# Mamba layer and attention layer on one core: fourteen Winograd weight pieces made on VectorE beside two attentions, second layer in pairs of images

## The chip, the cores and the metric

The kernel runs on one core of a Trainium2 chip, in float32. The metric is device microseconds of one execution, as the median of several runs. The engines are named as in the profile: PE is TensorE's matmul and PEld its weight load, DVE is VectorE, ACT is ScalarE, POOL is GpSimd, SP is SyncE, which here only issues DMA transfers.

## The reference

The input `x` is 4 x 512 x 32 x 32: 4 images, 512 channels, 1024 positions. Two layers follow each other, each with a group norm ahead of it and a residual around it.

```python
# layer 0: Mamba over the 1024 positions of each image
x = x + mamba(group_norm(x))
#   xn = layer_norm(tokens); xm, z = split(xn @ W_in)         512 -> 2 x 1024
#   xs = silu(causal_conv4(xm)); dt, Bm, Cm = xs @ W_x ...; dt = softplus(dt @ W_dt + b)
#   for each position: h = exp(dt * A) * h + (dt * xs) * Bm;  y = sum_s h * Cm    16 states
#   out = ((y + xs * D) * silu(z)) @ W_out                    1024 -> 512
# layer 1: attention over positions, between two 3x3 convolutions
x = x + pab(group_norm(x))
#   top, center = conv1x1(x)  (64 channels each);  bottom = conv3x3(x, w_bottom)  512 -> 512
#   map = softmax over all 1024*1024 entries of (center^T top)
#   out = conv3x3(x + map @ bottom^T, w_out)                  512 -> 512
```

## The kernel before

**Layer 0** is cut into 512 units: image `b`, channel block pair `e, h` (8 blocks of 128 channels), state `s` (16). A unit makes the decay `da` on ACT (L837), the product `dbx` of input and B on POOL or otherwise (L864), the scan on DVE (L889), the product with C, `da <- da * cbc`, mostly on POOL (L911) or on DVE (L905), and adds it up over the states by matmuls with the identity on PE into `y` (L918). The rows of B and C come as broadcasts by DMA on SP (`bbc`, `cbc`, 256 KB each). Gates, projections and the norms of the next image lie between the units.

The order is not left to the framework: every operation is a step of a list scheduler (`Plan`), which knows a time for each step, the size of each ring of buffers and a priority `prio` (unit numbers, 0 to 512). It replays the engines on its own clock, takes on each engine the ready step of the lowest priority, and writes the instructions in that order. Steps marked `fill` wait until no other step further than 17.64 behind them in priority is open.

**The weight pieces.** Both 3x3 convolutions are done as Winograd products, F(4) along rows and F(2) along columns: 6 x 4 transformed weight matrices of 512 x 512, kept in DRAM (`ub` for `w_bottom`, `uo` for `w_out`). They are made in layer 0 as fill work: `transform` (L1159) makes one of 16 pieces of a convolution (128 input channels x 128 output channels). On SP it loads the three rows of taps (192 KB each); ACT makes two scaled copies (L1177, L1178); POOL makes three additions on 128 x 768 (L1185, L1191, L1195) and nine on 128 x 256 (L1203 to L1205); SP stores the result in twelve transfers of 128 KB (L1212). The loop over 32 pieces gives the first `t0` = 7 the priority -5 and piece `k` behind them `tg * (k - t0)`, with `tg` = 18.5 units.

**Layer 1** is put in order by the framework from the order in the program. `scores(b)` makes the two 1x1 convolutions (`pt`, L1359), the score matrix (`psc`, L1380), the maximum and the exponentials; `conv3` (L1429) makes a 3x3 convolution: the six rows of transformed inputs in three pairs (1,2), (3,4), (0,5), the temporaries `e` to `l` on ACT and POOL, the sums `rr` and the transformed inputs `v` on DVE (L1488 to L1491), then for each of 24 weight matrices a load of 1 MB on SP into a ring of three buffers (`uw`, tag `u`, L1499) and four matmuls (L1503). `attend(b)` (L1546) has eight steps `k` of eight matmuls (`pat`, L1553), each followed by one DVE operation that adds the result to the normalised image (`xg`, L1566). `finish` adds the residual and stores the output; `last` does that for the last image, woven into its last convolution. `norm(b+1)` normalises the next image; its second half is run inside `attend(b)`. For the last image `by_chunk` makes the first inputs of the output convolution inside the attention, chunk by chunk. In the rest of the text `b1` is the first convolution of image 1 (`ub`) and `o0` the second of image 0 (`uo`); `v_b1` and `uw_b1` are their inputs and weights. The order of images is:

```python
st, rp = scores(0, xg)
for b in range(B):
    xb = conv3(f"b{b}", xg, ub, brow[0])
    ...                       # norm(b + 1) is run inside attend
    attend(b, xg, st, rp, xb, after, chunk)
    ...
    st, rp = scores(b + 1, image[b + 1])
    finish(b, conv3(f"o{b}", xg, uo, brow[1]))
```

Of the kernel before, what the change touches and what calls it, by code (L numbers as in the profile page):

```python
# [8 lines left out]
F32 = mybir.dt.float32  # L9
AF = mybir.ActivationFunctionType  # L10
ALU = mybir.AluOpType
# [4 lines left out]
P = 128  # L16
B, C, HH, WW = 4, 512, 32, 32
L = HH * WW
NCC = C // P
# [8 lines left out]
GS = 16  # L28


PRM = dict(pg=0.53, kt=2, ke=1, ka=-0.68, fl=0, fi=4.6, m0=48, n0=50.77, nl=2.05, c0=61.67, cg=6.03, p0=112, e0=6, eg=4.75, g0=78.98, gg=9.04, o0=13.03, og=5.23, dl=8.5, t0=7, tg=18.5, zl=11.5, f1=1.5)


class Buf:
# [137 lines left out]
def mamba_then_pab_kernel(  # L172
# [25 lines left out]
    nc = tc.nc  # L198
# [44 lines left out]

    NP6, NQ = 6, 4
    ub, uo = (
        [
            dram.tile([NP6, P, NCC, C], F32, tag=f"u_{n}_{q}", name=f"u_{n}_{q}")
# [23 lines left out]
    image = {}  # L273
# [6 lines left out]
    with ExitStack() as l0:  # L280
# [13 lines left out]
        QC = C // 4  # L294
# [932 lines left out]
            conv1_first(d, 0, -17 + 0.1 * d)  # L1227
            alone(silu(0, [d], slice(0, T)), -17 + 0.1 * d)
        params(0, -16, (0,))
        for k in range(2 * NPC):  # L1230
            u, src = ((ub, w_bottom), (uo, w_out))[k // NPC]
            transform(u, src, k % NPC, -5 if k < PRM['t0'] else PRM['tg'] * (k - PRM['t0']))

# [61 lines left out]
    with ExitStack() as l1:  # L1295
# [104 lines left out]

        shape = [P, NCC, TI, WW + 2]

        def by_chunk(name, xg):

            e, f = (
                tp.tile(shape, F32, tag="rt", name=f"{n}_{name}", bufs=4) for n in "ef"
            )
            r = tp.tile([P, 2, *shape[1:]], F32, tag="rr", name=f"rr_{name}_1", bufs=1)
            v = xp.tile([P, NQ, 2, NCC, P], F32, tag="v", name=f"v_{name}_1", bufs=2)

            def chunk(c):
                rows = [xg[:, c, a : a + 4 * TI - 3 : 4, :] for a in range(5)]
                for t, a in ((e, 2), (f, 1)):
                    nc.scalar.activation(t[:, c], rows[a], AF.Copy, scale=-4.0)
                    nc.gpsimd.tensor_add(t[:, c], t[:, c], rows[a + 2])
                nc.vector.tensor_add(r[:, 0, c], e[:, c], f[:, c])
                nc.vector.tensor_sub(r[:, 1, c], e[:, c], f[:, c])
                x = [r[:, :, c, :, a : a + 2 * TJ - 1 : 2] for a in range(4)]
                vq = [
                    v[:, q, :, c].rearrange("p n (i j) -> p n i j", j=TJ) for q in range(NQ)  # L1420
                ]
                nc.vector.tensor_sub(vq[2], x[2], x[1])  # L1422
                nc.vector.tensor_add(vq[1], x[1], x[2])
                nc.vector.tensor_sub(vq[0], x[0], x[2])
                nc.vector.tensor_sub(vq[3], x[1], x[3])

            return v, chunk

        def conv3(name, xg, u, bias, first=None, late=None):  # L1429

# [3 lines left out]
            def rows(a):  # L1434
                return xg[:, :, a : a + 4 * TI - 3 : 4, :]

            def tmp(n):
                return tp.tile(shape, F32, tag="rt", name=f"{n}_{name}", bufs=4)

            def flat(t):  # L1440
                return t.rearrange("p c i x -> p (c i x)")

            def inputs(pair):

                r = tp.tile([P, 2, *shape[1:]], F32, tag="rr", name=f"rr_{name}_{pair[0]}", bufs=1)
                r0, r1 = r[:, 0], r[:, 1]
                if pair == (1, 2):
                    e, f = tmp("e"), tmp("f")
                    nc.scalar.activation(e, rows(2), AF.Copy, scale=-4.0)
                    nc.scalar.activation(f, rows(1), AF.Copy, scale=-4.0)  # L1450
                    nc.gpsimd.tensor_add(e, e, rows(4))
                    nc.gpsimd.tensor_add(f, f, rows(3))
                    nc.vector.tensor_add(r0, e, f)
                    nc.vector.tensor_sub(r1, e, f)
                    return r
                if pair == (3, 4):
                    g, h = tmp("g"), tmp("h")
                    nc.gpsimd.tensor_sub(g, rows(4), rows(2))
                    nc.gpsimd.tensor_sub(h, rows(3), rows(1))
                    kept.extend((g, h))  # L1460
                    for o, w in ((r0, 2.0), (r1, -2.0)):
                        nc.vector.scalar_tensor_tensor(
                            flat(o), flat(h), w, flat(g), ALU.mult, ALU.add
                        )
                    return r
                g, h = kept
                k, l = tmp("k"), tmp("l")
                nc.gpsimd.tensor_sub(l, rows(0), rows(2))
                nc.gpsimd.tensor_sub(k, rows(5), rows(3))
                for o, a, w, s in ((r0, l, 4.0, g), (r1, h, -4.0, k)):  # L1470
                    nc.vector.scalar_tensor_tensor(
                        flat(o), flat(a), w, flat(s), ALU.mult, ALU.add
                    )
                return r
# [1 line left out]
            kept = []  # L1476
            y = [None] * 4
            for pair in PAIRS:
                if first and pair == (1, 2):
                    v = first  # L1480
                else:
                    r = inputs(pair)

                    v = xp.tile([P, NQ, 2, NCC, P], F32, tag="v", name=f"v_{name}_{pair[0]}", bufs=2)
                    rv = r.rearrange("p n c i x -> p (n c i) x")
                    x = [rv[:, :, a : a + 2 * TJ - 1 : 2] for a in range(4)]
                    vq = [v[:, q].rearrange("p n c (i j) -> p (n c i) j", j=TJ) for q in range(NQ)]
                    nc.vector.tensor_sub(vq[2], x[2], x[1])  # L1488
                    nc.vector.tensor_add(vq[1], x[1], x[2])
                    nc.vector.tensor_sub(vq[0], x[0], x[2])  # L1490
                    nc.vector.tensor_sub(vq[3], x[1], x[3])  # L1491
                ns = []
                for k, p in enumerate(pair):
                    m = {}
# [48 lines left out]
                nc.vector.scalar_tensor_tensor(f[3], f[3], 6.0, f[1], ALU.mult, ALU.add)  # L1543
            return y

        def attend(b, xg, st, rp, xb, between, chunk):  # L1546


            for k in range(NCC * NH):
                j, h = divmod(k, NH)  # L1550
                pt = ps.tile([P, C], F32, tag="ps", name=f"pat_{b}_{j}_{h}")
                for m in range(NMC):
                    nc.tensor.matmul(  # L1553
                        pt, st[m][:, 2 * P * j + h : 2 * P * (j + 1) : 2],
                        xb[m // 2][:, m % 2, :],
                        start=(m == 0), stop=(m == NMC - 1),
                    )
# [12 lines left out]
                if h and chunk:  # L1570
                    chunk(j)

        dst = [out[b].rearrange("(c p) h w -> p c (h w)", p=P) for b in range(B)]

# [23 lines left out]
        def finish(b, y):  # L1598

            for j in range(NCC):  # L1600
                o = load_sum(b, j, fp, "f4")
                for rr in range(2):
                    turn_back(b, j, o, y, rr)
                nc.scalar.dma_start(dst[b][:, j, :], o)

        def last(b, xg, v):

            o = [load_sum(b, j, xp, "st") for j in range(NCC)]

# [9 lines left out]
        xg = image[0]  # L1619
        st, rp = scores(0, xg)  # L1620
        for b in range(B):
            xb = conv3(f"b{b}", xg, ub, brow[0])
            after = norm(b + 1) if b + 1 < B else iter(())
            next(after, None)

            v, chunk = by_chunk(f"o{b}", xg) if b + 1 == B else (None, None)
            attend(b, xg, st, rp, xb, after, chunk)
            if b + 1 == B:
                last(b, xg, v)
                break  # L1630
            st, rp = scores(b + 1, image[b + 1])
            finish(b, conv3(f"o{b}", xg, uo, brow[1]))
            xg = image.get(b + 1)


# [55 lines left out]
```

## Time and profile before

| | us |
|---|---|
| three runs | 3073.21, 3081.69, 3087.27 |
| median | 3081.69 |
| the profiled execution | 3079.09 |
| its span in the trace | 3077.3 |
| layer 0, to about | 2044 |
| layer 1 | 1033 |
| mean granted PE clock | 0.972 |

The span runs from the first to the last instruction; 1.8 us lie around it. Layer 0 ends where the last residual sums of image 3 are made (DVE L1069, at 2044.5), and the first matmul of layer 1's first convolution stands at 2059.6. The busy time of each engine is summed over both layers, so its share of the span hides that the layers are limited by different engines; a stage is read in windows. The granted clock is the share of full speed at which PE was allowed to run.

### The profile page before, as it was taken

How to read it: one execution, taken by the hardware profiler on the slowest of the kernel's cores; microseconds unless marked ns; L12 is line 12 of the kernel's file. 1: busy time of each engine (PE TensorE's matmuls, PEld its weight loads, DVE VectorE, ACT ScalarE, POOL GpSimd, SP SyncE). 2: the span in 40 equal slices, each digit the busy share in tenths (PEclk: the TensorE clock that was granted, in tenths of full speed). 3: DMA queues.
4: the chain of work that ended last, by engine and by line, in shares of the span. 5: the costliest groups of instructions: out<-in, count | busy, mean ns of one | idle time of the engine just before them, and what ended most of it. 6: DMA issues, size and time to landing. Idle time of an engine off the chain costs nothing.

```text
span 3077.3 us, 36921 instructions
## 1 busy us (share of the span) xinstructions
PE 2789.0 (91%) x11896; PEld 1669.4 (54%) x11896; DVE 2290.1 (74%) x2989; ACT 1822.0 (59%) x3300; POOL 2125.4 (69%) x1197
## 2 busy tenths in 40 slices
PE   6788789999889999888999968879999999999998
PEld 2556566566666666666666656644444444444444
DVE  4579999888999988989988879985285375346344
ACT  4679878898888888788898879941120030030000
POOL 6989888899978899978889999952151143134222
PEclk9899899999999999999999989999999999999999
DMA  6756455577645577745567654448178458628827
GB/s 183 219 171 210 142 158 155 174 233 241 210 139 173 179 222 239 237 128 162 164 189 222 213 159 140 134 121 319 43 266 316 155 175 317 245 85 312 302 86 260
DMA packets 404537, 600.07 MB, mean 195 GB/s; under 512 B 47192, under 2 KB 246104, under 8 KB 379768
## 3 DMA queue, kind: packets, MB, share of 16 engines
q1 hardware_dynamic: 395536, 583.18, 59.8%
q10 hardware_dynamic: 8648, 14.26, 1.3%
q8 instruction: 95, 1.56, 0.2%
q14 instruction: 98, 0.80, 0.1%
q0 software_dynamic: 160, 0.26, 0.0%
HBM read 500.60 MB, written 96.99 MB: 194 GB/s over the span
## 4 chain that ended last, share of the span: by engine, by line
PE 40%; DVE 12%; ACT 6%; DMA 4%; POOL 4%; issue 3%; SPq 0%; DVEq 0%; POOLq 0%; ACTq 0%
PE m_o L1503 10%; PE m_b L1503 8%; PE pat L1553 7%; DVE da L889 5%; PE y L918 3%; PE po L402 2%; PE psc L1380 2%; PE u L875 2%; DMA uw_b<-u_b 2%; POOL da L911 2%; DVE dbx L889 2%; DVE u L889 1%; PE pz L402 1%; PE pp L728 1%; ACT sc L849 1%
## 5 line engine op out<-in xcount | busy, mean ns | idle before, releaser
L911 POOL TENSOR_TENSOR da<-da,cbc 128x1024 f32<-128x1024 f32 x328 | 773.2, 2368 | 114.7 <-DVE da L889 53.1
L849 ACT ACTIVATE sc<-dtxt,bt_sb 128x256 f32<-128x256 f32 x1312 | 578.1, 499 | 99.3 <-PE u L875 98.5
L837 ACT ACTIVATE da<-dt,a_sb 128x512 f32<-128x512 f32 x656 | 454.1, 716 | 78.8 <-PE y L918 62.8
L864 POOL TENSOR_TENSOR dbx<-dtx,bbc 128x1024 f32<-128x1024 f32 x184 | 434.4, 2373 | 10.6 <-DVE carry_sb L894 4.6
L889 DVE TENSOR_TENSOR_SCAN da<-da,carry_sb,u 128x512 f32<-128x512 f32 x328 | 403.1, 1262 | 42.4 <-PE u L875 40.1
L918 PE MATMUL y<-ident,da 128*128 128x128 f32 x2624 | 366.6, 284 | 72.1 <-POOL da L911 69.9
L889 DVE TENSOR_TENSOR_SCAN da<-da,u 128x512 f32<-128x512 f32 x328 | 397.9, 1213 | 31.0 <-PE u L875 29.0
L875 PE MATMUL u<-ident,sc 128*128 128x128 f32 x2624 | 389.2, 282 | 23.5 <-DVE da L889 14.8
L918 PEld LDWEIGHTS y<-ident,da 128*128 128x128 f32 x2624 | 309.4, 146 | 180.6 <-POOL da L911 132.3
L875 PEld LDWEIGHTS u<-ident,sc 128*128 128x128 f32 x2624 | 314.2, 145 | 113.5 <-issue 34.2
L1503 PE MATMUL m_b<-uw_b,v_b 128*128 128x512 f32 x768 | 337.6, 596 | 17.5 <-issue 8.3
L1503 PE MATMUL m_o<-uw_o,v_o 128*128 128x512 f32 x768 | 334.1, 595 | 4.5 <-DVE v_o L1422 4.1
L402 PE MATMUL pxm<-xt,winc 128*128 128x341 f32 (+4 forms) x768 | 251.0, 470 | 21.7 <-DVE xs L661 10.5
L1503 PEld LDWEIGHTS m_b<-uw_b,v_b 128*128 128x128 f32 x768 | 143.4, 190 | 204.1 <-issue 187.1
L402 PE MATMUL pz<-xt,winc 128*128 128x512 f32 x512 | 244.8, 599 | 8.8 <-DMA winc<-in_w_in_dram 2.5
L837 ACT ACTIVATE u<-dt,a_sb 128x512 f32<-128x512 f32 x368 | 245.5, 681 | 11.9 <-DVE da L889 6.7
L1503 PEld LDWEIGHTS m_o<-uw_o,v_o 128*128 128x128 f32 x768 | 145.6, 191 | 190.2 <-issue 181.7
L918 PE MATMUL y<-ident,dbx 128*128 128x128 f32 x1472 | 215.4, 285 | 36.0 <-DVE dbx L905 24.7
L918 PEld LDWEIGHTS y<-ident,dbx 128*128 128x128 f32 x1472 | 175.7, 147 | 88.2 <-DVE dbx L905 25.8
L1553 PE MATMUL pat<-y_b,st 128*128 128x512 f32 x512 | 221.7, 593 | 0.1
L661 DVE SCALAR_TENSOR_TENSOR xs<-pxm,cw_sb,xs 128x341 f32<-128x341 f32 (+8 forms) x288 | 163.6, 569 | 60.6 <-ACT xs L652 53.6
L1511 ACT ACTIVATE e_b<-m_b 128x512 f32<-128x512 f32 x24 | 14.3, 596 | 316.4 <-PE m_b L1503 300.0
(220 smaller groups left out, 4315.4 us busy)
## 6 DMA issues: line engine op xcount, KB each, us to landing
cbc<-bcd SPq DMA_DIRECT2D x512, 256.0 KB, 3.6
uw_b<-u_b SPq DMA_DIRECT2D x96, 1024.0 KB, 5.1
uw_o<-u_o SPq DMA_DIRECT2D x96, 1024.0 KB, 4.9
bbc<-bcd SPq DMA_DIRECT2D x184, 256.0 KB, 3.9
u_b<-work SPq DMA_DIRECT2D x192, 128.0 KB, 3.0
u_o<-work SPq DMA_DIRECT2D x192, 128.0 KB, 3.4
winc<-in_w_in_dram SPq DMA_DIRECT2D x72, 256.0 KB, 3.7
szd<-sz SPq DMA_DIRECT2D x32, 512.0 KB, 4.0
```

The lines of the kernel that those rows point to most:

```text
L402: lambda k=k, lhs=lhs, rhs=rhs: nc.tensor.matmul(p()[:, at : at + cols], lhs(), rhs(), start=(k == 0), stop=(k == n - 1)),
L661: nc.vector.scalar_tensor_tensor(u()[:, first:end], p()[:, first - k - at + before : n - k + before], cw[k], u()[:, first:end], ALU.mult, ...
L837: nc.scalar.activation(t, dt()[:, j], AF.Exp, scale=a_sb[:, at : at + 1])
L849: nc.scalar.activation(sc()[:, k], dtxt()[:, k], AF.Copy, scale=bt[:, at, s : s + 1])
L864: lambda: nc.gpsimd.tensor_mul(hc(), dtx(), b_bc().to_broadcast([P, 2, T])),
L875: nc.tensor.transpose(u()[:, k * P : (k + 1) * P], sc()[:, k, j, :], ident)
L889: nc.vector.tensor_tensor_scan(ht, *((hc()[:, j], u()) if on_act else (u(), hc()[:, j])), carry_sb[:, j, s : s + 1] if h else 0.0, ALU.mul ...
L911: lambda: nc.gpsimd.tensor_mul(hc(), hc(), c_bc().to_broadcast([P, 2, T])),
L918: nc.tensor.matmul(y[j]()[:, k, :], hc()[:, j, k * P : (k + 1) * P], ident, start=(s == 0 and k == 0), stop=(s == NS - 1 and k == NK - 1), ...
L1380: nc.tensor.matmul(pt, top[:, m * P : (m + 1) * P], center[:, h * T : (h + 1) * T], start=True, stop=True,)
L1503: nc.tensor.matmul(m[q], v[:, q, k, c, :], w[:, c, :], start=(c == 0), stop=(c == NCC - 1 and not extra),)
L1553: nc.tensor.matmul(pt, st[m][:, 2 * P * j + h : 2 * P * (j + 1) : 2], xb[m // 2][:, m % 2, :], start=(m == 0), stop=(m == NMC - 1),)
```

## The change

Three things change.

1. Layer 0 makes 18 of the 32 weight pieces instead of 32 (all 16 of `w_bottom` and `EARLY` = 2 of `w_out`), and `tg`, the distance in units between the priorities of two pieces, goes from 18.5 to 42.
2. Layer 1 goes by pairs of images, (0, 1) and (2, 3): scores, first convolution and attention of both, then the second convolution and the output of both. `by_chunk` is gone; `first_inputs` makes the first inputs of `o0` (or `o2`) ahead of the second attention of the pair. The norm of image 2 is run inside `o1`, behind its first inputs.
3. The other 14 pieces of `w_out` are made by a new function `piece`, seven in `attend(0)` and seven in `attend(1)`, one behind each `xg` from `k` = 1 on. A piece loads the same taps (three loads of 192 KB on SP) into a buffer of the ring of the transformed inputs (`v`, two buffers), makes six operations on 128 x 384 and three on 128 x 768 on DVE, the last three into a buffer of the ring of the weights (`u`, three buffers), and stores four parts of 384 KB on SP.

```diff
-PRM = dict(..., t0=7, tg=18.5, zl=11.5, f1=1.5)
+PRM = dict(..., t0=7, tg=42, zl=11.5, f1=1.5)
...
-    NP6, NQ = 6, 4
+    NP6, NQ, EARLY = 6, 4, 2
...
-        for k in range(2 * NPC):
+        for k in range(NPC + EARLY):
             u, src = ((ub, w_bottom), (uo, w_out))[k // NPC]
             transform(u, src, k % NPC, -5 if k < PRM['t0'] else PRM['tg'] * (k - PRM['t0']))
...
-        def by_chunk(name, xg):
...
+        def piece(k):
+
+            c, part = divmod(k, C // QC)
+            cs = slice(part * QC, (part + 1) * QC)
+            taps = w_out[c * P : (c + 1) * P, :, cs].rearrange("p (y x) o -> p y x o", y=3)
+            t = xp.tile([P, NQ, 2, NCC, P], F32, tag="v", name=f"w_{k}", bufs=2)
...
+            nc.sync.dma_start(g[:, 0], taps[:, 0])
+            nc.sync.dma_start(g[:, NP6 - 1], taps[:, 2])
+            nc.sync.dma_start(mid[:, 0], taps[:, 1])
...
+            dve.tensor_add(r[1], r[0], r[5])
+            stt(r[3], r[5], 4.0, r[0], ALU.mult, ALU.add)
+            dve.tensor_sub(r[2], r[1], m)
+            dve.tensor_add(r[1], r[1], m)
+            stt(r[4], m, -2.0, r[3], ALU.mult, ALU.add)
+            stt(r[3], m, 2.0, r[3], ALU.mult, ALU.add)
+            o = fp.tile([P, NCC, C], F32, tag="u", name=f"wo_{k}", bufs=3)
...
+            dve.tensor_add(o[:, 0], g[:, :, 0], g[:, :, 2])
+            dve.tensor_sub(o[:, 1], o[:, 0], g[:, :, 1])
+            dve.tensor_add(o[:, 0], o[:, 0], g[:, :, 1])
+            for q, part in enumerate((g[:, :, 0], o[:, 0], o[:, 1], g[:, :, 2])):
+                nc.sync.dma_start(uo[q].rearrange("n p c o -> p n c o")[:, :, c, cs], part)
...
-        def attend(b, xg, st, rp, xb, between, chunk):
+        def attend(b, xg, st, rp, xb, between, also):
...
-                if h and chunk:
-                    chunk(j)
+                for job in also[k : k + 1]:
+                    if job is not None:
+                        piece(job)
...
+        left = list(range(EARLY, NPC))
+        half = len(left) // 2
+        st, rp = scores(0, image[0])
+        for a in range(0, B, 2):
+            for b in (a, a + 1):
+                xb = conv3(f"b{b}", image[b], ub, brow[0])
+                also = [None] * (8 - half) + left[b * half : (b + 1) * half] if not a else []
+                after, v = iter(()), None
+                if b == a:
+                    after = norm(b + 1)
+                    next(after)
+                else:
+                    v = first_inputs(f"o{a}", image[a])
+                attend(b, image[b], st, rp, xb, after, also)
+                if b == a:
+                    st, rp = scores(b + 1, image[b + 1])
+            finish(a, conv3(f"o{a}", image[a], uo, brow[1], v))
+            if a + 2 == B:
+                last(a + 1, image[a + 1], None)
                 break
+            y = conv3(f"o{a + 1}", image[a + 1], uo, brow[1], mid=lambda: normed(a + 2))
+            finish(a + 1, y)
+            st, rp = scores(a + 2, image[a + 2])
```

More of the change, by code (lines that the diff above doesn't have):

```diff
@@ L28 @@
 GS = 16
-PRM = dict(pg=0.53, kt=2, ke=1, ka=-0.68, fl=0, fi=4.6, m0=48, n0=50.77, nl=2.05, c0=61.67, cg=6.03, p0=112, e0=6, eg=4.75, g0=78.98, gg=9.04, o0=13.03, og=5.23, dl=8.5, t0=7, tg=18.5, zl=11.5, f1=1.5)
+PRM = dict(pg=0.53, kt=2, ke=1, ka=-0.68, fl=0, fi=4.6, m0=48, n0=50.77, nl=2.05, c0=61.67, cg=6.03, p0=112, e0=6, eg=4.75, g0=78.98, gg=9.04, o0=13.03, og=5.23, dl=8.5, t0=7, tg=42, zl=11.5, f1=1.5)
 class Buf:
@@ L1401, in mamba_then_pab_kernel @@
         shape = [P, NCC, TI, WW + 2]
-        def by_chunk(name, xg):
[L1405 to L1427, printed above, removed]
@@ L1429, in conv3, with spread @@
-        def conv3(name, xg, u, bias, first=None, late=None):
+        def spread(name, p, r):
+            v = xp.tile([P, NQ, 2, NCC, P], F32, tag="v", name=f"v_{name}_{p}", bufs=2)
+            rv = r.rearrange("p n c i x -> p (n c i) x")
+            x = [rv[:, :, a : a + 2 * TJ - 1 : 2] for a in range(4)]
+            vq = [v[:, q].rearrange("p n c (i j) -> p (n c i) j", j=TJ) for q in range(NQ)]
+            nc.vector.tensor_sub(vq[2], x[2], x[1])
+            nc.vector.tensor_add(vq[1], x[1], x[2])
+            nc.vector.tensor_sub(vq[0], x[0], x[2])
+            nc.vector.tensor_sub(vq[3], x[1], x[3])
+            return v
@@ new lines, in tmp, with row_pair, first_inputs @@
+        def tmp(n, name):
+            return tp.tile(shape, F32, tag="rt", name=f"{n}_{name}", bufs=4)
+        def row_pair(name, p):
+            return tp.tile([P, 2, *shape[1:]], F32, tag="rr", name=f"rr_{name}_{p}", bufs=1)
+        def first_inputs(name, xg):
+            r = row_pair(name, 1)
+            ts = []
+            for n, a in (("e", 2), ("f", 1)):
+                t = tmp(n, name)
+                rows = [xg[:, :, k : k + 4 * TI - 3 : 4, :] for k in (a, a + 2)]
+                nc.scalar.activation(t, rows[0], AF.Copy, scale=-4.0)
+                nc.gpsimd.tensor_add(t, t, rows[1])
+                ts.append(t)
+            nc.vector.tensor_add(r[:, 0], *ts)
+            nc.vector.tensor_sub(r[:, 1], *ts)
+            return spread(name, 1, r)
@@ new lines, in piece @@
+        def piece(k):
[3 more added lines that the diff above has]
+            t = xp.tile([P, NQ, 2, NCC, P], F32, tag="v", name=f"w_{k}", bufs=2)
+            t = t.rearrange("p q n c t -> p (q n c t)").rearrange("p (r o) -> p r o", o=QC)
+            g, mid = (t[:, a : a + n].rearrange("p (r x) o -> p r x o", x=3) for a, n in ((0, 3 * NP6), (3 * NP6, 3)))
+            nc.sync.dma_start(g[:, 0], taps[:, 0])
+            nc.sync.dma_start(g[:, NP6 - 1], taps[:, 2])
+            nc.sync.dma_start(mid[:, 0], taps[:, 1])
+            r = [g[:, n].rearrange("p x o -> p (x o)") for n in range(NP6)]
+            m = mid[:, 0].rearrange("p x o -> p (x o)")
+            stt, dve = nc.vector.scalar_tensor_tensor, nc.vector
+            dve.tensor_add(r[1], r[0], r[5])
[5 more added lines that the diff above has]
+            o = fp.tile([P, NCC, C], F32, tag="u", name=f"wo_{k}", bufs=3)
+            o = o.rearrange("p c o -> p (c o)").rearrange("p (q r o) -> p q r o", o=QC, r=8)[:, :, :NP6]
+            dve.tensor_add(o[:, 0], g[:, :, 0], g[:, :, 2])
[3 more added lines that the diff above has]
+                nc.sync.dma_start(uo[q].rearrange("n p c o -> p n c o")[:, :, c, cs], part)
@@ L1434, in rows, with conv3 @@
+        def conv3(name, xg, u, bias, first=None, late=None, mid=None):
             def rows(a):
                 return xg[:, :, a : a + 4 * TI - 3 : 4, :]
-            def tmp(n):
-                return tp.tile(shape, F32, tag="rt", name=f"{n}_{name}", bufs=4)
             def flat(t):
@@ L1443, in inputs @@
             def inputs(pair):
-                r = tp.tile([P, 2, *shape[1:]], F32, tag="rr", name=f"rr_{name}_{pair[0]}", bufs=1)
+                r = row_pair(name, pair[0])
                 r0, r1 = r[:, 0], r[:, 1]
[L1447 to L1455, printed above, removed]
                 if pair == (3, 4):
-                    g, h = tmp("g"), tmp("h")
+                    g, h = tmp("g", name), tmp("h", name)
                     nc.gpsimd.tensor_sub(g, rows(4), rows(2))
@@ L1466, in inputs @@
                 g, h = kept
-                k, l = tmp("k"), tmp("l")
+                k, l = tmp("k", name), tmp("l", name)
                 nc.gpsimd.tensor_sub(l, rows(0), rows(2))
@@ L1478, in conv3 @@
             for pair in PAIRS:
-                if first and pair == (1, 2):
-                    v = first
-                else:
[L1482 to L1491, printed above, removed]
+                if pair == (1, 2):
+                    v = first or first_inputs(name, xg)
+                    if mid:
+                        mid()
+                else:
+                    v = spread(name, pair[0], inputs(pair))
                 ns = []
@@ L1617, in last, with normed @@
                 (nc.scalar, nc.sync)[j % 2].dma_start(dst[b][:, j, :], o[j])
[L1619 to L1629, printed above, removed]
+        def normed(b):
+            for _ in norm(b):
+                pass
+        left = list(range(EARLY, NPC))
[17 more added lines that the diff above has]
+                last(a + 1, image[a + 1], None)
                 break
-            st, rp = scores(b + 1, image[b + 1])
-            finish(b, conv3(f"o{b}", xg, uo, brow[1]))
-            xg = image.get(b + 1)
+            y = conv3(f"o{a + 1}", image[a + 1], uo, brow[1], mid=lambda: normed(a + 2))
+            finish(a + 1, y)
+            st, rp = scores(a + 2, image[a + 2])
 def kernel(**inputs):
```

## The prediction

> **What bounds the kernel now.** I read the busy shares first, then the chain of waits, then windows by stage, because a share is a mean over two layers with different limits. All windows below have the columns: stretch, length, busy PE, PEld, DVE, ACT, POOL, granted PE clock, DMA share, GB/s.
>
> ```profile
> PE 2789.0 (91%) x11896; PEld 1669.4 (54%) x11896; DVE 2290.1 (74%) x2989; ACT 1822.0 (59%) x3300; POOL 2125.4 (69%) x1197
> PE 40%; DVE 12%; ACT 6%; DMA 4%; POOL 4%; issue 3%; SPq 0%; DVEq 0%; POOLq 0%; ACTq 0%
> ```
>
> Over the whole span TensorE leads and POOL looks idle a third of the time. By stage it is otherwise:
>
> ```profile
> 640.00:880.00 240.00, 208.26 (x1161) 146.85 (x1159) 221.12 (x303) 205.67 (x379) 232.01 (x128) 0.96 0.70 214
> 880.00:1120.00 240.00, 227.35 (x1193) 152.43 (x1194) 217.54 (x297) 206.55 (x370) 205.51 (x118) 0.99 0.59 174
> 1120.00:1320.00 200.00, 176.18 (x972) 123.67 (x971) 180.34 (x248) 164.58 (x302) 193.27 (x108) 0.95 0.73 231
> 1560.00:1860.00 300.00, 264.27 (x1467) 181.78 (x1466) 242.85 (x305) 254.22 (x469) 286.81 (x156) 0.95 0.65 199
> 2044.00:3077.00 1033.00, 998.81 (x2405) 444.67 (x2404) 531.20 (x588) 136.63 (x244) 299.70 (x148) 0.99 0.61 218
> 2160.60:2216.30 55.70, 55.66 (x135) 25.74 (x134) 9.56 (x18) 0.47 (x2) 1.27 (x1) 1.00 0.07 25
> ```
>
> In the first layer (to 2044 us) four engines are all over 80% busy, and POOL is the fullest in three stretches, 740 us together (97%, 97%, 96%); between them TensorE is. The second layer (fifth row) is TensorE's alone, 97% busy, only 34 us idle. The last row is the first attention: 55.7 us, TensorE without a gap, VectorE 9.6, DMA 7%. So the change takes work from an engine that is first in part of a balanced stage, and puts it where VectorE and the queues are free but TensorE has no slack.
>
> **What a piece costs now.** POOL's rows (busy, mean ns | idle before):
>
> ```profile
> L1203 POOL TENSOR_TENSOR work<-work 128x256 f32<-128x256 f32 x96 | 70.2, 732 | 0.0
> L1185 POOL TENSOR_TENSOR work<-work 128x768 f32<-128x768 f32 x32 | 58.3, 1822 | 28.8 <-ACT work L1177 27.4 <-DMA u_b<-work 0.9 <-POOL da L911 0.4
> ```
>
> L1204 and L1205 are as L1203, L1191 and L1195 as L1185. A piece is 3 x 1.82 + 9 x 0.730 = 12.0 us of POOL, 1.03 us of ScalarE (two scales of 0.51) and 15 DMA issues on SP. Fourteen gone: 168 us of POOL, 14 of ScalarE, 210 issues at 0.44 us each. The order of instructions keeps pieces 0 to 7 where they are (until about 240 us); of the 24 behind them 10 stay, one of them in image 3.
>
> **The first layer's gain, by stage.** In a stretch where POOL is first, I let it shrink until the next engine has POOL's old share.
> - 640 to 880: pieces take 42.6 us, 14/24 of it goes, 24.9. VectorE stops it first: 221.1/0.967 = 228.7, a gain of 11.3.
> - 1120 to 1320: 21 us go; VectorE 180.3/0.966 = 186.7, gain 13.3.
> - 1560 to 1860: 48 us of pieces, 36 go (one stays); TensorE 264.3/0.956 = 276.4, gain 23.6. Here the mechanism is seen directly: at 1816 two 1.8 us operations and six 0.73 us ones stand ahead of a `dbx` product, VectorE waits 6.2 us for that and TensorE then 11.7 us.
> - Image 0 behind 240 us: about 2. Elsewhere POOL isn't first, but TensorE's waits for POOL's `da` and `dbx` there (240 to 640, 880 to 1120, 1320 to 1560) come to 19.5 + 2.9 + 4.3 = 26.7 us; I take half less the 2, 12.
>
> Sum 50 + 12 = **62 us**, which is 37% of the POOL time removed. The lower bound is the chain: on it, from 920 us to the layer's end, the three wide piece lines and a piece's load have 15.8 + 5.3 = 21 us; scaled by 2 to the part before and by 14/24, 25; less a little for dearer neighbours, 22. The upper bound: all POOL time removed in the three POOL-first stretches (82 us) plus the waits elsewhere, 100. ScalarE's 14 us and SP's issues count nothing: neither is first in any stretch.
>
> **The second layer's cost.** On VectorE a piece has six operations on 128x384 and three on 128x768. No row has these shapes; the nearest, 128x512 at 677 ns and 128x1088 at 1283 ns, give 1.052 ns for an element of a row: 6 x 0.542 + 3 x 0.946 = 6.1 us, 85 us in all. Seven of them (43 us), eight `xg` updates (6.0) and the norm (3.0) are 52 of the attention's 55.7 us: VectorE alone just fits, with no reserve.
>
> But a piece also needs its round trip: its loads go into the ring of the convolutions' inputs (`v`, 2 buffers), its result into that of the weights (`u`, 3 buffers). In the second attention SP has strictly: load piece k, store piece k (four stores, which wait for VectorE), load piece k+1. Each load therefore starts only when VectorE has ended the piece before. A 192 KB load lands 4.3 us after its issue, the third issue comes 0.9 us behind the first: 5.2, then 6.1 of VectorE, 11.3 us. If the loads wait in the DMA queue for the stores, 384 KB each in 512-byte packets (32 ns of one of 16 engines per packet by the busiest window of the trace, 1.6 us a store), up to 13.3. The first piece is done before the first `xg`; six more put the last one's end at about 79 to 90 us after the attention's start, and `w_14` and `w_15` stand on VectorE behind the last `xg`. What is queued behind: TensorE's next matmul is the first of `o0`, its 1 MB of weights come from the very buffer that these stores fill, so 3.4 us for the stores to land and 4.9 for the load follow, TensorE resumes at 87 to 101 us, and idles 32 to 46. I take **36**, near the low end, since DMA is 7% busy there, plus 2 for the restart: behind an 8.3 us gap at 2051 the granted clock was 0.54 for 3.5 us.
>
> In the first attention the next piece's loads stand partly ahead of the stores, so it is tighter: `w_8` and `v_b1` end behind the last `xg`, and the first weights of `b1` stand on SP behind `w_8`'s stores. TensorE has the scores of image 1 (22 us) but part of them waits for `xg`: **9** (bounds 4, one piece's tail; 18, a round trip and a weight load).
>
> Order of pairs: the same matmuls, and in the last image the 4.1 us wait for `v_o` goes: -4. Sum: 36 + 2 + 9 - 4 = **43 us** (28 to 62).
>
> **Two rules weighed.** In the second layer L1489, 128x1024 with two SBUF inputs, takes 3.6 us while POOL works and L1488, the same shape, 1.2 when it doesn't. The Trainium skill, SBUF — State Buffer, "Who interferes with whom", says that such a VectorE operation and a GpSimd one that reads SBUF shut each other out; it speaks against this change, as pieces have two SBUF inputs and POOL makes the next convolution's inputs in the attention. With eight POOL operations of 2.5 us it would add up to 20 us of VectorE time to an attention that is nearly full, and the sum would be about 3080. The first layer's scans, with POOL full, are steady at 1.21 to 1.27 us, so no speed-up of VectorE is counted there.
>
> The Trainium skill, TensorE: Matmul & The Clock Gate, "What's actually happening", lets the clock fall after a few idle microseconds and rise after as long at work; the 0.54 for 3.5 us agrees with it, and by it each long gap costs some 1.7 us instead of my 2 for both.
>
> **Sum.** The profiled execution took 3079.1 us (span 3077.3, 1.8 around it), 2.6 under the median of the runs, 3081.7. 3079 - 62 + 43 = **3060 us**, 0.7% under the median.
>
> **The rivals.**
> 1. *Slower: the first layer isn't bound by POOL.* In image 1 (592 to 1078) VectorE has 444.7 and TensorE 441.6 of 486 us, both 91%, as POOL; the chain gives POOL 4% of the span. Then only the chain's 22 us come back: 3079 - 22 + 43 = 3100. It decides where the gain is under 28. Against it: 97% in three stretches, and waits of 11.7 us with pieces ahead.
> 2. *No change: the attentions cost more*, 62, by 13.3 us a piece or by blocked VectorE operations: 3079 - 62 + 62 = 3079.
> 3. *The whole POOL time comes back*, 100, as the scheduler refills the stretches: 3079 - 100 + 43 = 3022. Against: VectorE and TensorE are at 91% there.
> 4. *It doesn't do what it says*: two pieces lie behind the second attention, not beside it. The 36 count that already; if the first attention is strung out like the second, 46 us idle in each, it is 3079 - 62 + 92 - 4 = 3105.
>
> **How the numbers follow.** About 0.5% (15 us) is what a measurement of this kernel can tell from no change, so faster is under 3066, slower over 3097. Forecast 0.40, own range 3042 to 3078, of it 0.32 faster and 0.08 same; rival 3, 0.15 faster; rival 2, 0.10 same; rival 1, 0.28, of it 0.23 slower and 0.05 same; rival 4's bad end, 0.07 slower. Together 0.47, 0.23, 0.30. The range takes in rivals 1 and 3 with a margin of 7 to 9: 3013 to 3107, leaving out 0.2.
>
> **What would show it.** Right: the layer's end (2044 now) at about 1982; POOL under 90% in the three stretches; second layer about 1076 long, with one TensorE gap of over 30 us behind the second attention that ends on a load of `uw_o` and a smaller one behind the first. Wrong: the layer's end over 2020 (rival 1) or under 1950 (rival 3); a VectorE piece over 9 us (blocked by POOL); no gap behind the second attention.

## The result, and the profile after

The changed kernel takes 3099.66 us (median of 5 runs, 3096.44 to 3105.09), the kernel before 3078.81 (median of 5). The ratio is 1.0065, interval 1.0044 to 1.0086: **slower by about 20 us**. The forecast, 3060 and faster, went the wrong way; the time lies in the range and on rival 1 (3100).

The profiled execution took 3099.67 us, its span is 3097.9. The last residual sum of layer 0 (DVE L1069) stands at 2024.3 where it stood at 2044.5, so layer 0 won **20.2 us**; the rest is 3097.9 - 2024.3 = 1073.6 us long where it was 1032.8, so layer 1 lost **40.8**. The prediction had 62 and 43. The cost was near, the gain was three times too large.

The page of the changed kernel, busy times and the chain:

```profile
PE 2785.9 (90%) x11896; PEld 1663.7 (54%) x11896; DVE 2364.3 (76%) x3097; ACT 1807.3 (58%) x3265; POOL 1963.7 (63%) x1023
PE 45%; DVE 20%; ACT 10%; DMA 6%; issue 4%; POOL 4%; SPq 0%; DVEq 0%; POOLq 0%; ACTq 0%
```

POOL lost 162 us of work, VectorE won 74, as the sums had it. The same windows as before the change, with the second layer last:

```profile
640.00:880.00 240.00, 207.84 (x1136) 143.48 (x1135) 220.09 (x300) 204.11 (x371) 201.11 (x98) 0.95 0.62 192
880.00:1120.00 240.00, 223.91 (x1173) 150.79 (x1172) 211.31 (x288) 198.17 (x354) 182.97 (x97) 0.98 0.51 151
1120.00:1320.00 200.00, 180.12 (x1010) 125.13 (x1007) 186.25 (x258) 169.06 (x310) 177.53 (x88) 0.97 0.70 222
1560.00:1860.00 300.00, 274.03 (x1585) 189.99 (x1584) 265.49 (x339) 271.38 (x503) 286.31 (x143) 0.99 0.63 192
2024.00:3097.00 1073.00, 1003.03 (x2405) 448.95 (x2403) 606.32 (x696) 135.57 (x238) 301.31 (x142) 0.97 0.69 238
```

The first row decides it. From 640 to 880 POOL went from 232.0 us to 201.1, and TensorE, VectorE and ScalarE did no more in these 240 us than before (207.8 for 208.3, 220.1 for 221.1, 204.1 for 205.7). POOL simply stood idle for the 31 us that the pieces had taken. The two rows behind it cancel: a little less work in the second (VectorE 211.3 for 217.5), a little more in the third (186.3 for 180.3). In the fourth row it is otherwise: TensorE 274.0 for 264.3, VectorE 265.5 for 242.9, more work in the same time.

The scans of layer 0 can be counted (two a unit), which gives the time at which each unit is reached. Unit 400, early in image 3, is reached at 1654.0 before and 1655.8 after: no gain in three images, although POOL has 130 us less work on pieces there (225.5 us between 240 and 1560 before, 95.5 after). Between units 400 and 416 the change wins 2.5 us, between 416 and 464 it wins 19.4, and behind 464 nothing.

In layer 1 TensorE's waits, of the kernel changed (us in total, times, longest):

```profile
PE m_o L1518 <- DMA uw_o<-u_o: 34.0, 3, 33.3
PE m_b L1518 <- issue: 8.3, 1, 8.3
PE pm_l L1334 <- DVE mv_l L1328: 7.0, 1, 7.0
PE m_b L1518 <- DMA uw_b<-u_b: 6.8, 4, 5.1
PE pt L1359 <- DVE xg L1581: 3.2, 1, 3.2
```

The first is the gap behind the second attention, the fourth (5.1 of it) and fifth are those behind the first; the second was there before, the third is new and belongs to the order of pairs (see below). The timeline of TensorE at the second attention (start, duration, idle before in brackets):

```profile
2334.55 34.07 PE L1568 MATMUL pat<-y_b,st 128*128 128x512 f32 x79
2401.94 10.08 PE L1518 MATMUL m_o<-uw_o,v_o 128*128 128x512 f32 x16 [33.32 <-DMA uw_o<-u_o]
```

and of SP's queue in the same stretch (start and duration of the issues):

```profile
2343.79 0.95 SPq L1461 DMA_DIRECT2D u_o<-w  x2
2346.31 1.35 SPq L1461 DMA_DIRECT2D u_o<-wo  x2
2348.02 0.38 SPq L1443 DMA_DIRECT2D w<-in_w_out_dram  x1
...
2355.52 0.96 SPq L1461 DMA_DIRECT2D u_o<-w  x2
...
2396.34 83.19 SPq L1514 DMA_DIRECT2D uw_o<-u_o  x24
```

A piece's first stores at 2343.8, the next one's at 2355.5: a piece every 11.7 us. The weights of `o0` go out behind the last stores, at 2396.3, and TensorE, done with the attention at 2368.6, goes on at 2401.9.

### The profile page after: what moved, and what is told of

It is laid out like the page before. It is cut to its first block, busy times and chain, and to the rows that moved or that the text cites. A ratio compares the mean times of both kernels' runs of the same rounds, so it can differ in the third digit from the quotient of the medians.

```text
span 3097.9 us, 36662 instructions
## 1 busy us (share of the span) xinstructions
PE 2785.9 (90%) x11896; PEld 1663.7 (54%) x11896; DVE 2364.3 (76%) x3097; ACT 1807.3 (58%) x3265; POOL 1963.7 (63%) x1023
## 4 chain that ended last, share of the span: by engine, by line
PE 45%; DVE 20%; ACT 10%; DMA 6%; issue 4%; POOL 4%; SPq 0%; DVEq 0%; POOLq 0%; ACTq 0%
PE m_b L1518 10%; PE m_o L1518 10%; DVE da L889 7%; PE y L918 5%; PE po L402 4%; PE pat L1568 4%; PE u L875 3%; ACT sc L849 3%; DVE u L889 2%; PE pxm L402 2%; DVE dbx L889 2%; POOL da L911 2%; ACT da L837 2%; PE psc L1380 2%; PE pp L728 2%
## 5 line engine op out<-in xcount | busy, mean ns | idle before, releaser
L889 DVE TENSOR_TENSOR_SCAN da<-da,carry_sb,u 128x512 f32<-128x512 f32 x328 | 402.4, 1262 | 42.6 <-PE u L875 40.1
L918 PE MATMUL y<-ident,da 128*128 128x128 f32 x2624 | 360.0, 282 | 73.6 <-POOL da L911 70.8
L889 DVE TENSOR_TENSOR_SCAN da<-da,u 128x512 f32<-128x512 f32 x328 | 397.8, 1213 | 20.2 <-PE u L875 19.4
L402 PE MATMUL pxm<-xt,winc 128*128 128x345 f32 (+4 forms) x768 | 258.3, 479 | 34.7 <-DVE xs L661 10.7
L918 PE MATMUL y<-ident,dbx 128*128 128x128 f32 x1472 | 209.1, 281 | 24.6 <-DVE dbx L905 12.3
L402 PEld LDWEIGHTS pxm<-xt,winc 128*128 128x128 f32 x768 | 145.4, 200 | 117.5 <-issue 40.9
```

Of the source, the lines that this page charges most:

```text
L402: lambda k=k, lhs=lhs, rhs=rhs: nc.tensor.matmul(p()[:, at : at + cols], lhs(), rhs(), start=(k == 0), stop=(k == n - 1)),
L889: nc.vector.tensor_tensor_scan(ht, *((hc()[:, j], u()) if on_act else (u(), hc()[:, j])), carry_sb[:, j, s : s + 1] if h else 0.0, ALU.mul ...
L918: nc.tensor.matmul(y[j]()[:, k, :], hc()[:, j, k * P : (k + 1) * P], ident, start=(s == 0 and k == 0), stop=(s == NS - 1 and k == NK - 1), ...
```

## The experiments

Times are medians; the kernel before was run beside each group, so the ratio is the safer number. "Layer 0" and "layer 1" are cut at the last L1069 as above, in one profiled execution each. Executions with the same layer 0 ended it up to 4 us apart (2020.4 and 2024.3 below), and one execution of the first experiment by 6 us in the part that the edit does not touch. So differences of a few us in layer 0 are not read.

| run | us | ratio to before, interval | layer 0 | layer 1 |
|---|---|---|---|---|
| before | 3078.8 | | 2044.5 | 1032.8 |
| the change | 3099.7 | 1.0065 (1.0044 to 1.0086) | 2024.3 | 1073.6 |
| without the work of pieces 28 to 31 | 3060.0 | 0.9954 (0.9936 to 0.9973) | 2030.9 | 1036.1 |
| without the work of pieces 8 to 27 | 3063.7 | 0.9959 (0.9944 to 0.9973) | 2028.7 | 1032.9 |
| pieces closer, 14.5 units | 3087.0 | 1.0035 (1.0021 to 1.0050) | 2055.6 | 1033.1 |
| order of pairs alone | 3068.3 | 0.9969 (0.9953 to 0.9985) | 2042.8 | 1023.6 |
| four pieces on VectorE | 3051.9 | 0.9904 (0.9880 to 0.9928) | 2025.2 | 1025.6 |
| first inputs late | 3071.2 | 0.9974 (0.9960 to 0.9989) | 2020.4 | 1044.6 |
| the change at 18.5 units | 3095.2 | 1.0045 (1.0025 to 1.0064) | 2019.9 | 1074.7 |
| without the work of pieces 8 to 31 | 3049.8 | 0.9901 (0.9879 to 0.9923) | 2017.2 | 1031.6 |
| products moved to POOL, two of four | 3078.3 | 1.0003 (0.9988 to 1.0017) | 2026.5 | 1047.5 |
| products moved to POOL, one of four | 3068.1 | 0.9970 (0.9954 to 0.9986) | 2018.3 | 1048.0 |
| two pieces on VectorE | 3053.5 | 0.9910 (0.9886 to 0.9934) | 2029.9 | 1024.8 |
| one piece on VectorE | 3055.3 | 0.9921 (0.9901 to 0.9942) | 2035.6 | 1025.0 |

**Theory and rival at the start.** "Place": the pieces lie in POOL's idle time in images 0 to 2 and cost only in image 3, where the next image's convolutions and norms are missing. "Amount": each microsecond of POOL is worth the same everywhere.

**1. Pieces of image 3 left out.** The kernel before, with this in `transform`, for `k >= 28`:

```diff
+            if copy:                      # loads and stores stay, ACT and POOL do nothing
+                for rows in (slice(1, 4, 2), slice(2, 5, 2), slice(0, 6, 5)):
+                    for q in range(NQ):
+                        ...  step("SP", ..., dma_start(dst, ends()[:, 0:2, min(q, 2)]))
+                return
```

> The kernel before, with the POOL and ACT work of pieces 28 to 31 left out (their loads and stores stay; the weights stored are the taps themselves). These are the pieces that lie in image 3. Theory 'place' (pieces cost only where no next image fills the other engines, in image 3): layer 0 ends 16 to 21 us earlier than 2044, the time about 3060. Rival 'amount' (each us of POOL work removed is worth the same anywhere, by the result 20 us for 168): 48 us x 0.12, about 6 us, 3073.

14 us faster, and by the units it wins 20 us between 416 and 464 (from 6.3 behind to 14.1 ahead). "Amount" (6 us) is out for these four.

**2. Pieces of images 0 to 2 left out.** The same for `8 <= k < 28`.

> The kernel before, with the POOL and ACT work of pieces 8 to 27 left out (their loads and stores stay), 240 us of POOL work in images 0 to 2; pieces 28 to 31 in image 3 stay. 'Place': no change beyond 8 us, 3071 to 3087. 'Amount': 240 x 0.12, about 29 us, 3050. The prediction's stage sums (37% of what is removed) would give 3079 - 89, about 2990.

12.6 us faster for 240 us of POOL work, 0.05 us per us: against 0.3 for the four above. "Place" had said at most 8, "amount" 29, the prediction's way of reckoning 89. None was right, "place" was nearest. Of the 15.8 us that layer 0 wins here, 10.0 lie ahead of unit 128, in image 0, for which the prediction had about 2; units 192 to 384 take 741.7 us for 744.8. The windows of this run in the stretch of the first row above, and in the next:

```profile
640.00:880.00 240.00, 211.68 (x1155) 147.02 (x1154) 221.01 (x303) 200.50 (x365) 181.82 (x82) 0.96 0.70 216
880.00:1120.00 240.00, 224.60 (x1204) 150.50 (x1203) 217.86 (x297) 207.04 (x372) 175.20 (x79) 0.99 0.57 173
```

POOL from 97% to 76% busy, VectorE unchanged at 92%, the pace unchanged: units 128 to 192 take 224.2 us with the pieces and 222.5 without.

**3. Pieces closer together.** The kernel before with one number changed:

```diff
-PRM = dict(..., tg=18.5, ...)
+PRM = dict(..., tg=14.5, ...)
```

> The kernel before with one number changed, the distance of the pieces' priorities, 18.5 to 14.5: all 32 pieces stay on POOL, but the last has priority 348 and none is left for image 3 (from 384 on). 'Place': layer 0 ends 16 to 21 us earlier, the time about 3060, below both kernels. 'Amount': the same POOL work, 3079. The prediction's reading (POOL full in images 1 and 2) makes it slower, since the pieces stand closer there: 3079 + 10 or more.

This fell against "place" (11 us slower) and went as the prediction's reading had it, and for a reason worth having. Image 3 did win, 23 us between units 384 and 512, but images 0 to 2 lost 33. By units (windows of the kernel before, then of this run; units 32 to 64, 128 to 192, 272 to 304):

```profile
255.00:374.00 119.00, 96.05 (x544) 69.87 (x542) 111.64 (x158) 103.60 (x190) 114.62 (x64) 0.91 0.61 186
631.00:855.00 224.00, 200.83 (x1108) 141.22 (x1106) 205.51 (x278) 189.77 (x351) 216.69 (x119) 0.95 0.75 229
1166.00:1276.00 110.00, 102.58 (x568) 70.33 (x567) 97.68 (x126) 91.08 (x169) 106.37 (x62) 0.98 0.74 236
```

```profile
257.00:385.00 128.00, 96.81 (x546) 69.69 (x545) 112.66 (x159) 105.61 (x195) 121.72 (x69) 0.92 0.63 186
642.00:877.00 235.00, 208.51 (x1115) 141.51 (x1114) 205.40 (x277) 194.85 (x360) 227.03 (x130) 0.95 0.74 226
1194.00:1308.00 114.00, 107.27 (x575) 73.06 (x574) 98.47 (x127) 91.77 (x170) 112.05 (x68) 0.97 0.77 234
```

The same units, 24 us longer (9 + 11 + 4), and POOL busy 23.1 us more (7.1 + 10.3 + 5.7): work *added* to POOL here cost its full time. (Over all units up to 384 it is 32.8 us for 35.7 us more of pieces.) Work *taken away* here (experiment 2) won 2 + 1 + 7 us for 74.6 us of POOL less (20.3 + 32.9 + 21.3). POOL stood at 96 to 97% in these windows, and that reads as a corner, not a slope: more work costs nearly all of its time, less work gives little back. (Each of these kernels also has an order of its own from the scheduler, which no run here holds fixed.)

**4. The order of pairs alone.** The changed kernel with all 32 pieces in layer 0:

```diff
-    NP6, NQ, EARLY = 6, 4, 2        ... tg=42
+    NP6, NQ, EARLY = 6, 4, 16       ... tg=18.5
```

> The changed kernel with all 32 pieces made in layer 0 at the old distance of 18.5 and none on VectorE: the order of pairs alone. Layer 0 as before (2044). The prediction gave the order alone -4 us in layer 1 (the wait for v_o of the last image): 1029 for 1033, the time 3075. Rival: the order itself costs in layer 1 (the norm of image 2 later, no conv beside the scores), 3085 or more, and the VectorE pieces are then less than the 43 us.

Layer 1 is 9.2 us shorter, more than the 4 predicted. Before, TensorE waited there 8.3 us in 12 places for `uw_b`, 4.1 for `v_o` and 3.8 for `top`, 16.2 together; here 0.5 is left of them, and a 5.9 us wait for the norm of image 2 (`pm_l`) is new. So the fourteen pieces cost layer 1 not 40.8 but 1073.6 - 1023.6 = 50 us.

**5. Four pieces instead of fourteen.** The change, with exactly the pieces of image 3 taken out of layer 0, behind the first `xg` of each attention:

```diff
-    NP6, NQ, EARLY = 6, 4, 2        ... tg=42
+    NP6, NQ, EARLY = 6, 4, 12       ... tg=18.5
-                also = [None] * (8 - half) + left[b * half : (b + 1) * half] if not a else []
+                also = [None] + left[b * half : (b + 1) * half] if not a else []
```

> The change done for four pieces instead of fourteen: EARLY = 12 and the old distance of 18.5, so that exactly the pieces of image 3 leave layer 0 and those of images 0 to 2 stay where they were; two in each attention, behind the xg of k = 1 and 2; order of pairs as in the changed kernel. Theory 'place': layer 0 ends 14 to 20 us earlier as in the run without these pieces; two pieces of 11.7 us each end long before the attention's 55 us, no gap behind it, layer 1 about 1024 as with the order alone; together 3047 to 3053, below both kernels. Rival: any piece on VectorE delays the first weights of the next convolution by its stores, 10 us or more in each attention: 3065 or more.

As "place" had it: 3051.9 us, **28 us below the kernel before and 48 below the change**, the lowest median of the versions that do all of the work (two pieces and one, below, aren't told apart from it by their intervals). TensorE goes from the second attention straight into `o0`:

```profile
2308.94 48.32 PE L1568 MATMUL pat<-y_b,st 128*128 128x512 f32 x112
2357.10 7.03 PE L1518 MATMUL m_o<-uw_o,v_o 128*128 128x512 f32 x16
```

**6. What sets the 11.7 us of a piece.** The first inputs of `o0` hold one of the two buffers of the ring `v` throughout the second attention.

```diff
-                    v = first_inputs(f"o{a}", image[a])
+                    v = None
```

> The changed kernel, but the first inputs of o0 (and o2) are made inside that convolution, not ahead of the second attention, so that the pieces have both buffers of the ring v in the attention. Theory 'buffer' (a piece's loads wait for the one buffer left): the period of a piece falls from 11.7 us to 7 or 8, the gap behind the second attention from 33 to 20 or less although the first inputs now come behind it; layer 1 about 1060, the time about 3085. Theory 'queue' (the loads wait in the DMA queue behind the stores): the period stays at 11 to 12, the gap 33 or more plus the first inputs, 3100 or more.

The buffer, not the queue: layer 1 is 29 us shorter. From TensorE's timeline of this run:

```profile
2316.59 48.32 PE L1568 MATMUL pat<-y_b,st 128*128 128x512 f32 x112
2371.16 9.87 PE L1518 MATMUL m_o<-uw_o,v_o 128*128 128x512 f32 x16 [6.25 <-DMA uw_o<-u_o]
```

33.3 us have become 6.3. VectorE begins its pieces in twos, at 2312.5 and 2315.3, 2330.2 and 2333.0, 2347.6 and 2351.0: 17.6 us for two, 8.8 each, where the expectation had 7 or 8. The operations themselves took 0.55 and 0.95 us in both runs. So it was mostly the buffer that an early result sat in, and not the stores in the DMA queue, that kept the loads; VectorE still waits 4.8 to 4.9 us for them ahead of each two, and what sets that was not tried.

**7. The wider distance undone.** The change with `tg` at 18.5 again.

> The changed kernel with tg back at 18.5: 18 pieces in layer 0 as in the change, but at the places of the kernel before (the last at priority 185, early in image 1), none behind it. It tells whether the wider distance of 42 cost time in images 0 to 2, where the changed kernel lost 15 us between units 48 and 256 with fewer pieces. Theory 'place' with position: units 64 to 256 as before or better, layer 0 ends at 2005 to 2015, the time about 3083. Rival (scatter of the order, or of one execution): layer 0 ends at 2024 as with 42, 3100.

4 us less in layer 0 than with 42, the rival's value within the scatter of one execution. The theory's first part held, units 64 to 256 took 738.5 us as before (737.7) where the change took 751.7. But up to unit 64 the change was 7 us quicker, and behind 384 3 us, so that little is left of it at the end. That the change won nothing up to unit 400 is such a sum of parts, too. Whether the place of the ten kept pieces is worth anything stays open.

**8. All pieces behind the eighth left out.** Experiments 1 and 2 together.

> The kernel before, with the POOL and ACT work of all pieces from 8 on left out (loads and stores stay): 288 us of POOL work. If the two parts add up (15 us in images 0 to 2, 15 in image 3, as measured apart): layer 0 ends at about 2013, the time 3046 to 3050. If POOL were what bounds the stage throughout (the prediction's reading, 37%): 106 us, 2973. If the layer has a limit of its own behind both: no more than each alone, 3060.

The parts add up, with 288 us of POOL work gone. So with the rest of the kernel as it is, POOL's pieces behind the eighth cost 9 to 11% of their time (27.3 us in layer 0, 30.5 by the ratio), not 37%. The largest group of POOL, in the kernels before, changed, and here (busy, mean ns | idle before it, most of it ended by):

```profile
L911 POOL TENSOR_TENSOR da<-da,cbc 128x1024 f32<-128x1024 f32 x328 | 773.2, 2368 | 114.7 <-DVE da L889 53.1
```

```profile
L911 POOL TENSOR_TENSOR da<-da,cbc 128x1024 f32<-128x1024 f32 x328 | 773.8, 2366 | 224.7 <-DVE da L889 86.5
```

```profile
L911 POOL TENSOR_TENSOR da<-da,cbc 128x1024 f32<-128x1024 f32 x328 | 773.9, 2367 | 328.5 <-DVE da L889 122.1
```

POOL's time turned into waiting: 115, 225 and 329 us ahead of these products. VectorE's scan ended 53, 87 and 122 us of it, and the copy of the scan's last column (L894) another 20, 80 and 96.

**9 and 10. Is VectorE what bounds images 1 and 2, then?** Base: the change with `tg` at 18.5 and `v = None`. Part of VectorE's products with C goes to POOL, which is now idle there:

```diff
-        C_ON_DVE = [(1, 5, 9, 13)] * (B - 1) + [(5, 13)]
+        C_ON_DVE = [(1, 5, 9, 13), (5, 13), (5, 13), (5, 13)]        # and (3, 8, 13) in images 1 and 2
```

> What bounds images 1 and 2 when POOL is free? Base: the changed kernel with tg at 18.5 and the first inputs of o0 made late (both were measured apart: layer 0 ends at 2020, layer 1 takes 1045, together about 3067). In images 1 and 2, where no piece is left on POOL behind unit 185, two of the four products with C per group that VectorE makes (L905) go to POOL: 32 a product and image, 0.66 x 2 us of VectorE and 2.37 of POOL for each of 16 units an image, 21 us less on VectorE and 38 more on POOL. Theory 'VectorE is the next limit': the images shorten by 10 to 20 us each, about 3035. Theory 'no engine alone, the loop of PE, VectorE, ACT and POOL': within 10 us of 3067, or slower, as POOL comes back to 97%.

> The same base with one of the four products moved in images 1 and 2: 11 us less on VectorE and 19 more on POOL an image. 'VectorE next': 5 to 10 us an image, about 3052. 'No engine alone': 3060 to 3070.

3078 and 3068, where the base adds up to 3067: not VectorE alone. The base itself was not run, only its two parts. With two products moved, units 160 to 192, where pieces still lie on POOL, lost 9 us against the run at 18.5 (the window 640 to 880 has POOL at 236.2 of 240); from 192 to 384, with less on VectorE, only 4 came back, though POOL was busy 77 to 88% of the time there (from 880 to 1560) and not at 97%.

**11 and 12. Which piece of image 3?** As experiment 5, with `EARLY` = 14 and 15: two pieces, or only the last, on VectorE.

> As the run with four pieces on VectorE, but only the last two (priorities 425 and 444), one in each attention, and 30 in layer 0. Theory 'one stall' (the 20 us of image 3 come from the place at 1800 to 1850 where the last piece stands in one block ahead of the products): layer 0 ends at about 2025 as without four, the time 3050 to 3055. Rival 'each piece of image 3 costs the same, 5 us': layer 0 ends at 2034, the time about 3061.

> As before with only the last piece (priority 444) on VectorE, in the first attention, and 31 in layer 0. 'One stall': layer 0 ends at about 2026, 3051 to 3056. 'Each the same': 2039, about 3066.

"One stall" it is, nearly: by the ratios the order alone wins 9.5 us, with one piece 24.3, with two 27.7, with four 29.6 (what the ratio lacks to 1, times 3078.8; each +-5 to 7). In the profiled executions units 416 to 464 take 173.6 us with the order alone, 160.9, 156.5 and 155.0 with one, two and four pieces on VectorE, 154.6 in the change. **The last of 32 pieces alone is worth about 13 to 15 us of the 20;** the 5 of the three ahead of it are no more than the noise. The ends of layer 0 speak less clearly: with one piece 2035.6 lies nearer to "each the same" (2039) than to "one stall" (2026), with two 2029.9 lies between them, but the execution profiled with one piece (3062.4 us) was the slowest of its four. Where the last piece stands could be read in the kernel before. Its chain of waits in order of time (start, us, what) says:

```profile
1809.67 1.79 POOL work L1185
...
1813.76 2.31 POOL da L911
1816.06 1.80 POOL work L1191
1817.93 1.81 POOL work L1195
...
1822.06 1.74 DMA u_o<-work
1824.27 2.35 POOL dbx L864
```

The piece is put down in two blocks, with one product between them, and a `dbx` that VectorE and then TensorE wait for stands behind it. Such blocks alone don't make a piece dear: most of the pieces behind the eighth are spread over 19 to 48 us, but 11, 17, 18 and 24 took 14.6 to 14.8 us from first to last operation, as the last one did (14.7), and the chain around piece 24 (1290.6 to 1305.2) has none of its operations. What sets the last one apart by "place" is that no next image's convolutions and norms lie beside it; that fits, but no run changed it alone. In the run with one piece on VectorE POOL goes from 1804.5 on through products alone, and 1800 to 1850 has TensorE at 42.2 us for 31.4.

## Why the prediction was right or wrong

- *What bounds the kernel.* That layer 1 is TensorE's was right, that POOL bounds three stretches of layer 0 was wrong for taking work away, though right for adding it (experiment 3). The 97% held fill work, and it could go almost without effect: experiment 2 took 50 us of POOL's 232 out of one stretch, and the units there (128 to 192) took 1.7 us less.
- **The step that failed: the layer's gain by stage.** "In a stretch where POOL is first, I let it shrink until the next engine has POOL's old share" takes a busy share for a limit. Its terms were 11.3, 13.3 and 23.6, with 2 and 12 for the rest. Up to unit 400 the changed kernel won nothing (-1.7 us) where 38.6 were reckoned; in image 3 it won 22 for 23.6. This last term has nearly the right size by another cause: not the 36 us of POOL in 300, but mostly one stall, that of the last piece, which the trace showed and the prediction named ("seen directly"). The right size of this term is luck. (In the first stretch the pieces measure 42.2 us, not 42.6; its term doesn't depend on that.)
- *The lower bound*, 22 us from the chain, was the answer (20.2), and rival 1 gave 3100 for 3099.7. It came from the wide operations of some three pieces and one load on the chain, scaled as if spread evenly; in order of time the last piece alone, with its narrow operations, has 11.4 us there, 9.7 of POOL and 1.7 of a store. That the scaled number fits so well is in part luck.
- *The rival's point "VectorE and TensorE are at 91%"* was evidence that moved too little weight. What limits images 0 to 2 isn't VectorE by itself either (experiments 9 and 10); a loop through PE, VectorE, ACT and POOL, unit after unit, is a guess that fits these runs, but was not shown by any.
- *A piece on VectorE*, 0.54 and 0.95 us per operation: measured 0.55 and 0.95 where POOL is quiet. Right.
- *The second attention*, 36 us of 32 to 46: measured 33.3. The period of 11.3 to 13.3 was 11.7. The cause left undecided (load and store in strict order on SP) is the held buffer.
- *The restart*, 2 us: 3.0, since 16 matmuls took 10.08 us for 7.03. The granted clock was 0.50 for 3.5 us and 0.64 for the next 3.5. The Trainium skill, TensorE: Matmul & The Clock Gate, "What's actually happening", has TensorE at half its clock for about the first 3.4 us of work after an idle time. The first 3.5 us agree with that, the next 3.5 don't; an estimate from its figure gives a loss of 1.7 us.
- *The first attention*, 9 us of 4 to 18: 3.2 + 5.1 = 8.2. Right.
- *VectorE and POOL shutting each other out.* The Trainium skill, SBUF — State Buffer, "Who interferes with whom", says that a VectorE operation with two SBUF inputs and a GpSimd one that reads SBUF block each other. The trace agrees: in the first attention six operations of the pieces ran 2.2 to 2.9 us instead of 0.55 or 0.95 while POOL made the inputs of `b1`, 11.8 us more in all. It was weighed as up to 20 us of VectorE time; how much of the 11.8 is in the 8.2 us of gaps behind that attention was not tried.
- *The order*, -4: -9.2. Too small, since the 8.3 us of waits for `uw_b` and the 3.8 for `top` were not looked for. The 43 came so near in part because two errors went against each other: the pieces cost 50 us for 47, the order won 9.2 for 4. Sum of layer 1: 33.3 + 3.0 + 8.2 - 9.2 = 35.3 of the 40.8 measured; 5 us are in smaller waits that were not followed.

## What to carry to other kernels

Before reckoning what it is worth to take work off an engine, ask how that work came to be there: fill work makes its engine look full, and taking 288 us of it away gave back 27 here. Look for what of it stands on the chain, read in order of time, not as a share. Such an engine can be at a corner: removing 75 us from it won 10, adding 23 cost 24. And when one piece of the moved work accounts for most of the gain, move that piece: one of fourteen brought 13 to 15 of the 20 us, at no cost that could be seen where it went (layer 1 took 1025.0 us, with the order alone 1023.6).

## What was not expected of the hardware

After an idle time of 33.3 us TensorE was granted 0.50 of its clock for 3.5 us and 0.64 for 3.5 more. The length of the idle time doesn't decide how long that lasts: after 6.25 us in experiment 6 it was 0.50 and 0.70, after 33.9 us in experiment 7 0.50 and 0.82, and after 8.3 us in the kernel before 0.54 for 3.5 us, then 1.00.
